# Rows of 768 columns instead of 704 for the intermediate of a quantized feed-forward block

## The chip, the cores and the metric

The kernel runs on one core of a Trainium2 chip. The metric is device time in microseconds (us) of one execution, taken as the median of repeated runs; lower is better. The engines have short names in the profile: PE is TensorE's matmul, PEld its weight load, DVE VectorE, ACT ScalarE, POOL GpSimd and SP the sync engine, which issues the DMAs.

## The reference, cut to what matters

A tensor x of 8 sequences, 1024 rows each, width 256, passes four residual blocks; each adds a function of a layer norm of x:

```python
x = x + linear_attention_layer(layernorm(x))   # block 1, with its own FFN of width 1024 (Gelu)
x = x + relu_ffn(layernorm(x))                 # block 2, width 1024
x = x + softmax_attention(layernorm(x))        # block 3, one head of width 256
x = x + fp4_ffn(layernorm(x))                  # block 4

def fp4_ffn(x):                                # w_gate, w_up: (704, 256), w_down: (256, 704)
    gate = fp4_linear(x, w_gate)
    y = fp4_linear(x, w_up)
    h = silu(gate) * y                         # 704 columns
    return fp4_linear(h, w_down)
```

`fp4_linear` first rounds both operands, in blocks of 16 along the contracted dimension, to a grid of eight magnitudes times the block's scale, and then multiplies. The intermediate `h` has 704 columns, five times 128 and 64. All data are fp32.

## The kernel before

Rows go through in chunks of 128 (64 chunks) and, for blocks 1 and 2, in groups of 4 chunks, the 16 flows. Five generators describe the work: `linear_attention` (block 1's attention, for each flow four `front`s that normalise x, and four `linear_chunk`s), `dense` (the two FFNs of width 1024, with weights streamed from memory in tiles `w_ff`), `softmax_and_fp4` (`soft_chunk`, blocks 3 and 4 of a chunk), and two that prepare weights.

A planner, `Plan`, interleaves them. Each generator yields what its next step needs (an engine, tiles, PSUM banks, a free buffer of a kind); `Plan.run` takes the step that can start first by a table of costs in `Plan.took`, with PE first among equals. `Queue` ties the instructions of each engine to that order, so each engine executes a fixed list and waits in it by semaphores. `TILES` says how many buffers each kind of tile has. Only the order comes from the planner; on the chip every engine runs as soon as its semaphores allow. The planner's price of a matmul follows from the columns of its output alone; it has no term for a change of the array's shape.

Names that occur later:

- `load_x` issues the DMA of a chunk of x into a tile of kind `x`; `front` takes it (statistics `ln_st`, `ln_mv` on DVE, `ln_ve` and `ln_rstd` on POOL, then n on DVE) and gives the buffer back. x has four buffers, one for each chunk of a flow. After its own chunk c, `front` loads chunk c + 4.
- `n0T` is the transposed n of a whole flow, which the projections (`n0T, wqkv`) read once all four fronts are through.
- `soft_chunk` makes, for a chunk, the attention (`n2T`, `qT`, `prob`, `probT`, `vt`), then block 4: gate and up products (`wgT`, `wuT` with `xqT`), the intermediate `hid` of 128x704 in one of three buffers, its rounding by `fp4`, six transposes of `hid` through PSUM into `hqT`, and six matmuls with `wdT` that accumulate the down product, 128x256.
- `hsum`, `qz` and `sc` are operands of block 1's matmuls that use 32 columns or 32 rows of the array at a time.

Around the change, the sixth piece of `hid` has 64 columns. Its transpose therefore gives 64 rows, which are copied out of PSUM by themselves, and the sixth matmul contracts over 64 rows:

```python
INTER_TILES = [(t * P, min(P, INTER - t * P)) for t in range((INTER + P - 1) // P)]
```

Every operation is issued through one helper, so all instructions of the profile stand at line L268 and are told apart by tile names.

Of the kernel before, what the change touches and what calls it, by code (L numbers as in the profile page):

```python
# [9 lines left out]
F32 = mybir.dt.float32  # L10
# [6 lines left out]
P = 128  # L17
D = 256
# [4 lines left out]
INTER = 704  # L23
V_PADS = 5
W_FF = 5
RES = 10
# [3 lines left out]
G = 4  # L30
GT = G * P
LN_EPS = 1e-5
ATT_EPS = 1e-6
BANKS = 8
INTER_TILES = [(t * P, min(P, INTER - t * P)) for t in range((INTER + P - 1) // P)]


# [2 lines left out]


TILES = {
    "x": (4, D, F32),
    "n0": (2, D, F32),
    "lin": (5, D, F32),
    "flow": (9, 512, F32),
# [3 lines left out]
    "soft": (5, D, F32),  # L50
    "prob": (7, 512, F32),
    "rows": (4, D, F32),
    "hid": (3, INTER, F32),
    "q_c": (2, INTER, BF16),
}

# [1 line left out]
class Plan:  # L58
# [27 lines left out]
    def bank(self, tile_):  # L86
        name = tile_.tensor.name
        self.used[name] = 0.0
        if len(self.banks) == BANKS:
            old = min((b for b in self.banks if b not in self.held), key=lambda b: self.used[b])  # L90
# [5 lines left out]
    def banks_free(self, count):  # L96

        if len(self.banks) + count <= BANKS:
            return 0.0
        times = sorted(self.used[b] for b in self.banks if b not in self.held)  # L100
        k = count - (BANKS - len(self.banks)) - 1
        return times[k] if k < len(times) else None
# [9 lines left out]
    def drop(self, *tiles):  # L112

        for tile_ in tiles:
            name = tile_.tensor.name
            kind = self.kind[name]
            self.live[kind].remove(name)
            self.slots[kind].append(self.used[name])

    def slot_free(self, kind):  # L120
        slots, live = self.slots.get(kind, []), self.live.get(kind, ())
        if len(live) + len(slots) < TILES[kind][0]:
            return 0.0
        return min(slots) if slots else None
# [76 lines left out]
    def pe(self, *tiles, **kw):  # L201
        return self.need("tensor", tiles, **kw)

    def dve(self, *tiles, **kw):
        return self.need("vector", tiles, **kw)

    def act(self, *tiles, **kw):
        return self.need("scalar", tiles, **kw)

    def dma(self, *tiles, **kw):  # L210
        return self.need("sync", tiles, **kw)
# [75 lines left out]
def block_stack_kernel(ctx: ExitStack, tc: tile.TileContext, a: dict, out: bass.AP):  # L287
# [20 lines left out]
    plan = Plan(tc, tc.nc)  # L308
    nc, pe, dve, act, dma = plan, plan.pe, plan.dve, plan.act, plan.dma
    x_dram = a["L0_attn_inputs"]  # L310
    B, L, _ = x_dram.shape
    NCH = L // P
    NG = NCH // G

    const = ctx.enter_context(tc.tile_pool(name="const", bufs=1))
# [4 lines left out]
    ps = ctx.enter_context(  # L320
        tc.tile_pool(name="ps", bufs=BANKS, space=bass.MemoryType.PSUM)
    )


    def mm_bank():
        bank = ps.tile([P, 512], F32, tag="bank", name="bank")
        plan.bank(bank)
        return bank

    def tr_bank():  # L330
        return mm_bank().rearrange("p (k t) -> p k t", k=4)
# [6 lines left out]

    def make(kind, name=None):
        bufs, width, dtype = TILES[kind]  # L340
        t = wk.tile([P, width], dtype, tag=kind, name=name or kind, bufs=bufs)
        plan.take(kind, t)
        return t

    def kept(shape, name, bufs):
        t = big.tile(shape, F32, tag=name, name=name, bufs=bufs)
        return t

    def small(shape, name, bufs=4):
        t = sm.tile(shape, F32, tag=name, name=name, bufs=bufs)  # L350
        return t
# [17 lines left out]
    ident = const.tile([P, P], F32, name="ident")  # L369
# [59 lines left out]
    for i in range(V_PADS):  # L429
        v = const.tile([P, H, 32], F32, name=f"v_pad{i}")  # L430
        nc.gpsimd.memset(v, 0.0)
        v_pads.append(v)


    def load_x(c):
        x = make("x")
        s, i = divmod(c, NCH)
        nc.sync.dma_start(out=x, in_=x_dram[s, i * P : (i + 1) * P, :])
        return x

    xs = {c: load_x(c) for c in range(G)}

    wqkv = const.tile([P, 2, 3 * D], F32, name="wqkv")
    bqk1 = const.tile([P, 4], F32, name="bqk1")
# [27 lines left out]
    wgT = const.tile([P, 2, INTER], F32, name="wgT")  # L472
    wuT = const.tile([P, 2, INTER], F32, name="wuT")
    wdT = const.tile([P, len(INTER_TILES), D], F32, name="wdT")


    def ln_stats(src):
# [10 lines left out]
    def layernorm(kind, src):  # L488
        mean, rstd = ln_stats(src)
        dst = yield from fresh(kind, dve(rstd), "n")  # L490
        nc.vector.tensor_scalar(dst, src, mean, rstd, ALU.subtract, ALU.mult)
        return dst
# [11 lines left out]
    def turned(srcs):  # L504

        bank = tr_bank()
        for i, src in enumerate(srcs):
            nc.tensor.transpose(bank[:, i, :], src, ident)
        return bank[:, : len(srcs), :]

    def halves(t):
        return [t[:, 0:P], t[:, P : 2 * P]]
# [51 lines left out]
    def fp4_weights():  # L564
        pieces = []
        for name, dstT in (("L1_ffn_w_gate", wgT), ("L1_ffn_w_up", wuT)):
            for r0, rows in INTER_TILES:
                turns = [(dstT[:, k, r0 : r0 + rows], k * P, P) for k in range(2)]
# [94 lines left out]
    def head_sums(prods):  # L663

        bank = mm_bank()[:, :P]
        for b, prod in enumerate(prods):
            for t in range(G):
                nc.tensor.matmul(
                    bank[32 * t : 32 * t + 32, :],
                    lhsT=hsum[:, b, :],  # L670
                    rhs=prod[:, t * P : (t + 1) * P],
                    start=b == 0,
                    stop=b == 3,
                    skip_group_check=True,
                )
        return bank
# [20 lines left out]
    def running(out, cur, carry, b, first, last):  # L697
# [16 lines left out]
    count = {  # L714
        "halves": 0,
        "dense": 0,
        "acc": 0,
        "res": 0,
        "v": 0,
        "scored": 0,  # L720
        "attended": 0,
        "linear": 0,
# [27 lines left out]
    def linear_group(p):  # L750
# [8 lines left out]

        def front(i):  # L760
            c = p * G + i
            x = xs.pop(c)
            yield dve(x, when=lambda: count["res"] < RES)
            count["res"] += 1
            rc = groups[p]["res"][i] = kept([P, D], "res", RES)
            n0 = yield from layernorm("n0", x)
            plan.drop(x)
            nc.gpsimd.tensor_tensor(rc, n0, bo, ALU.add)
            yield pe(n0, banks=1)
            bank = turned(halves(n0))  # L770
            plan.drop(n0)
            yield act(bank)
            nc.scalar.copy(n0T[:, :, i * P : (i + 1) * P], bank)
            fronts.append(i)
            if c + G < B * NCH:
                need = dma()
                need.fresh = "x"
                yield need
                xs[c + G] = load_x(c + G)

        fronts = []
        yield dve(at=p, when=lambda: count["v"] == p * G)
# [7 lines left out]
        for b in (2, 0, 3, 1):  # L790
            yield pe(n0T, banks=1)
            bank = mm_bank()
            for k in range(2):
                nc.tensor.matmul(
                    bank,
                    lhsT=wqkv[:, k, b * P : (b + 1) * P],
                    rhs=n0T[:, k, :],
# [20 lines left out]
        bank = head_sums(prods)  # L818
# [8 lines left out]
        for n, b in enumerate((2, 0, 3, 1)):  # L827
# [12 lines left out]
        bank = head_sums(prods)  # L840
# [11 lines left out]
        bank = mm_bank()[:, 0:1]  # L852
        nc.tensor.matmul(
            bank, lhsT=front_rows, rhs=total, start=True, stop=first
# [8 lines left out]
        ahead = small([P, 1], "ahead", 2)  # L863
# [24 lines left out]
        bank = tr_bank()  # L888
# [323 lines left out]
    def soft_chunk(cc):  # L1212
        s, c = divmod(cc, NCH)
        g, i = divmod(c, G)
# [4 lines left out]
        bank = mm_bank()  # L1219
        for e in range(2):  # L1220
            for k in range(2):
                nc.tensor.matmul(
                    bank[:, e * P : (e + 1) * P],
                    lhsT=wqk[:, k, e * P : (e + 1) * P],
                    rhs=n2T[g][:, k, i * P : (i + 1) * P],
# [10 lines left out]
        for kb in range(NG):  # L1236
            yield pe(qT, banks=1)
            bank = mm_bank()
            plan.keep(bank)
            for e in range(2):  # L1240
                nc.tensor.matmul(
                    bank, lhsT=qT[:, e, :], rhs=n2T[kb][:, e, :], start=e == 0, stop=e == 1
# [19 lines left out]
        for kb in range(NG):  # L1262
            yield pe(prob[kb], banks=1, at=at + 0.25)
            bank = turned([prob[kb][:, j * P : (j + 1) * P] for j in range(G)])
# [9 lines left out]
        bank = mm_bank()  # L1274
        for j in range(NCH):
            nc.tensor.matmul(
                bank[:, :D],
                lhsT=probT[j // G][:, j % G, :],
                rhs=vt[j // G][:, j % G, :],
# [12 lines left out]
        bank = turned(halves(n))  # L1292
# [3 lines left out]
        hid = None  # L1296
        for j0 in range(0, INTER, INTER // 2):
# [3 lines left out]
            for bank, wT in ((gb, wgT), (ub, wuT)):  # L1301
                for k in range(2):
                    nc.tensor.matmul(
                        bank,
                        lhsT=xqT[:, k, :],
                        rhs=wT[:, k, cols],
# [3 lines left out]
            if hid is None:  # L1310
                hid = yield from fresh("hid", act(gb))
# [8 lines left out]
        hqT = []  # L1320
        for half in range(2):
            yield pe(hid, banks=1, at=at + 0.75)
            tiles = INTER_TILES[4 * half : 4 * half + 4]
            bank = tr_bank()
            for k, (f0, rows_) in enumerate(tiles):
                nc.tensor.transpose(bank[:rows_, k, :], hid[:, f0 : f0 + rows_], ident)
            hqT.append((yield from fresh("prob", act(bank), "hqT")))
            hqT[half] = hqT[half].rearrange("p (k t) -> p k t", k=4)
            if half == 0:
                nc.scalar.copy(hqT[0], bank)  # L1330
            else:
                for k, (f0, rows_) in enumerate(tiles):
                    nc.scalar.copy(hqT[1][:rows_, k, :], bank[:rows_, k, :])
        yield pe(*hqT, banks=1)
        bank = mm_bank()
        for k, (f0, rows_) in enumerate(INTER_TILES):
            nc.tensor.matmul(
                bank[:, :D],
                lhsT=hqT[k // 4][:rows_, k % 4, :],
                rhs=wdT[:rows_, k, :],  # L1340
                start=k == 0,
                stop=k == len(INTER_TILES) - 1,
            )
# [63 lines left out]
```

## Time and profile before

| what | value |
|---|---|
| median of 6 runs | 2788.08 us (2783.82 to 2788.32) |
| the profiled execution | 2788.23 us |
| its span, first to last instruction | 2786.5 us |
| mean granted TensorE clock | 0.982 |
| busy: PE, DVE, ACT, POOL | 95%, 70%, 45%, 20% |
| ACT table loads | 314, 1283 ns each |
| `wdT, hqT` matmul records | 768, of them 128 with 64 rows |
| eviction of `hqT`, first half | 128x512, 585 ns each |
| eviction of `hqT`, second half | 128x128, 266 ns, and 64x128, 263 ns |

A row of groups names engine, operation, the tile written and those read, for PE the rows*columns of the array, the shape and the count; then busy time and mean time of one in ns, then the idle time of the engine just before and what ended it. Matmuls are pipelined and the profile models their ends, so the duration of one record is longer than the distance from its start to the next start. A matmul in fp32 leaves two records, a transpose one.

### The profile page before, as it was taken

What the parts mean: (1) busy time and instruction counts of PE and PEld (TensorE: products, weight loads), DVE (VectorE), ACT (ScalarE), POOL (GpSimd) and SP (SyncE); (2) the same over time, 40 slices, a digit from 0 to 9 for tenths busy, and PEclk for the clock granted to TensorE, in tenths of its full rate; (3) what the DMA queues carried; (4) which work ended last, traced back from release to release, by engine and by line L of the source; (5) the groups of instructions that cost most, each with busy time, mean ns of one, the idle gap of its engine ahead of it and who ended that gap; (6) DMA issues with size and microseconds to landing.
All of it is one profiled execution on the core that took longest, in us unless ns stands there. A gap on an engine that the chain in (4) does not pass through costs nothing.

```text
span 2786.5 us, 42805 instructions
## 1 busy us (share of the span) xinstructions
PE 2647.9 (95%) x15276; PEld 2019.3 (72%) x15276; DVE 1950.9 (70%) x4403; ACT 1255.3 (45%) x2482; POOL 557.9 (20%) x1100
## 2 busy tenths in 40 slices
PE   3978999999999999999999999999999999999997
PEld 1767777777777777777777777777777777777665
DVE  6877676785867768586685867678586766846565
ACT  2424343545444363544545455354544445444342
POOL 1323222121221211122121221212122121111000
PEclk7989999999999999999999999999999999999998
DMA  3234232222323222231222322132232312222000
GB/s 106 79 94 135 76 97 65 89 66 74 97 63 92 70 73 75 77 106 57 84 70 69 98 72 93 52 98 65 71 93 67 97 60 78 71 73 85 21 12 14
DMA packets 283204, 211.43 MB, mean 76 GB/s; under 512 B 23921, under 2 KB 270705, under 8 KB 282993
## 3 DMA queue, kind: packets, MB, share of 16 engines
q1 hardware_dynamic: 282992, 208.71, 25.0%
q8 instruction: 122, 2.00, 0.3%
q14 instruction: 90, 0.73, 0.1%
HBM read 189.74 MB, written 18.87 MB: 75 GB/s over the span
## 4 chain that ended last, share of the span: by engine, by line
PE 76%; DVE 13%; DMA 4%; ACT 4%; issue 2%; POOL 1%; SPq 1%; DVEq 0%; ACTq 0%; POOLq 0%
PE bank L268 76%; DVE prod L268 4%; DMA spread<-packed 2%; ACT L268 2%; DVE n L268 1%; DVE hid L268 1%; DVE spread L268 1%; DMA w_ff<-in_L_ffn_w_dram 1%; DVE ln_st L268 1%; ACT q_c L268 1%; DMA packed<-flow 1%; DVE u L268 1%; DVE x_amax L268 1%; SPq L268 1%; DVE div L268 0%
## 5 line engine op out<-in xcount | busy, mean ns | idle before, releaser
L268 PE MATMUL bank<-half,w_ff 128*128 128x256 f32 x2048 | 535.6, 384 | 16.6 <-DMA w_ff<-in_L_ffn_w_dram 13.4
L268 PE MATMUL bank<-w_ff,hidden 128*128 128x256 f32 x2048 | 527.2, 382 | 0.0
L268 PEld LDWEIGHTS bank<-half,w_ff 128*128 128x128 f32 x2048 | 381.2, 192 | 88.4 <-issue 26.0
L268 ACT ACT_TABLE_LOAD x314 | 402.9, 1283 | 78.2 <-PE bank L268 69.5
L268 PEld LDWEIGHTS bank<-w_ff,hidden 128*128 128x128 f32 x2048 | 368.1, 191 | 67.1 <-issue 24.2
L268 POOL TENSOR_SCALAR ln_ve<-ln_mv 128x1 f32<-128x1 f32 x384 | 89.1, 232 | 1320.6 <-DVE ln_mv L268 1309.7
L268 ACT ACTIVATE hidden<-bank,c_L_ffn_b 128x256 f32<-128x256 f32 x256 | 121.2, 473 | 339.9 <-PE bank L268 339.5
L268 PE MATMUL bank<-n2T,qT 128*128 128x512 f32 x512 | 241.6, 594 | 1.0 <-ACT qT L268 1.0
L268 PE MATMUL bank<-vt,probT 128*128 128x256 f32 x1024 | 234.1, 382 | 2.1 <-DVE probT L268 2.1
L268 DVE TENSOR_TENSOR hid<-hid,bank 128x352 f32<-128x352 f32 x128 | 65.8, 514 | 241.2 <-PE bank L268 160.3
L268 POOL TENSOR_TENSOR ln_rstd<-ln_ve,neghalf 128x1 f32<-128x1 f32 x384 | 225.9, 588 | 32.0
L268 PEld LDWEIGHTS bank<-vt,probT 128*128 128x128 f32 x1024 | 194.7, 192 | 42.6 <-issue 11.7
L268 DVE TENSOR_TENSOR sc<-bank,triu 128x512 f32<-128x512 f32 x256 | 161.9, 681 | 54.8 <-PE bank L268 54.8
L268 PE MATMUL bank<-wdT,hqT 128*128 128x256 f32 (+1 forms) x768 | 193.5, 394 | 0.8 <-ACT hqT L268 0.8
L268 ACT ACTIVATE hidden<-bank,c_L_attn_b 128x256 f32<-128x256 f32 x256 | 121.4, 474 | 146.0 <-PE bank L268 144.5
L268 PE MATMUL bank<-wgT,xqT 128*128 128x352 f32 x512 | 177.5, 469 | 1.6 <-ACT xqT L268 1.5
L268 PE MATMUL bank<-wuT,xqT 128*128 128x352 f32 x512 | 174.5, 464 | 0.0
L268 PEld LDWEIGHTS bank<-wdT,hqT 128*128 128x128 f32 (+1 forms) x768 | 141.5, 193 | 42.2 <-issue 23.7
L268 POOL TENSOR_TENSOR xr<-xr,b_L_attn_ln_b 128x256 f32<-128x256 f32 x64 | 54.3, 869 | 488.6 <-DMA xr<-in_L_attn_inputs_dram 488.6
L268 PEld LDWEIGHTS bank<-n2T,qT 128*128 128x128 f32 x512 | 93.0, 190 | 72.4 <-issue 63.2
L268 PEld LDWEIGHTS bank<-wuT,xqT 128*128 128x128 f32 x512 | 98.5, 192 | 55.2 <-issue 1.7
L268 PEld LDWEIGHTS bank<-wgT,xqT 128*128 128x128 f32 x512 | 92.7, 190 | 47.6 <-issue 12.8
(174 smaller groups left out, 4381.3 us busy)
## 6 DMA issues: line engine op xcount, KB each, us to landing
w_ff<-in_L_attn_W_dram SPq DMA_DIRECT2D x512, 128.0 KB
w_ff<-in_L_ffn_w_dram SPq DMA_DIRECT2D x512, 128.0 KB
spread<-packed SPq DMA_DIRECT2D x96, 256.0 KB
x<-in_L_attn_inputs_dram SPq DMA_DIRECT2D x64, 128.0 KB
xr<-in_L_attn_inputs_dram SPq DMA_DIRECT2D x64, 128.0 KB
rows<-res SPq DMA_DIRECT2D x64, 128.0 KB
rows<-rows SPq DMA_DIRECT2D x64, 128.0 KB
out_dram<-y SPq DMA_DIRECT2D x64, 128.0 KB
```

The lines of the kernel that those rows point to most:

```text
L268: ins = method(*args, **kw)
```

## The change

The tiles of the intermediate get 768 columns, whose last 64 are zeros, and the last 64 rows of the sixth tile of `wdT` are zeros too. Then all six transposes are of 128x128, the second half of `hqT` is evicted by one copy of 128x256 instead of two copies, and all six matmuls contract over 128 rows. Gate, up and the rounding still work on 704 columns.

So that the zeros are written once, the three `hid` tiles become fixed tiles, zeroed in their last columns at the start, and `make` hands out the one that was used longest ago (`Plan.oldest`). The room comes from `x`, which has three buffers instead of four. With three, the first three chunks are loaded at the start, `front` loads chunk c + 3 after its own, and a front waits until its chunk has been loaded.

```diff
@@ -32,6 +32,7 @@
 LN_EPS = 1e-5
 ATT_EPS = 1e-6
 BANKS = 8
+INTER_PAD = -(-INTER // P) * P
 INTER_TILES = [(t * P, min(P, INTER - t * P)) for t in range((INTER + P - 1) // P)]
 
 
@@ -40,7 +41,7 @@
 
 
 TILES = {
-    "x": (4, D, F32),
+    "x": (3, D, F32),
     "n0": (2, D, F32),
     "lin": (5, D, F32),
     "flow": (9, 512, F32),
@@ -50,7 +51,7 @@
     "soft": (5, D, F32),
     "prob": (7, 512, F32),
     "rows": (4, D, F32),
-    "hid": (3, INTER, F32),
+    "hid": (3, INTER_PAD, F32),
     "q_c": (2, INTER, BF16),
 }
 
@@ -116,6 +117,14 @@
             kind = self.kind[name]
             self.live[kind].remove(name)
             self.slots[kind].append(self.used[name])
+
+    def oldest(self, kind, tiles):
+
+        live = self.live.get(kind, ())
+        return min(
+            (t for t in tiles if t.tensor.name not in live),
+            key=lambda t: self.used.get(t.tensor.name, 0.0),
+        )
 
     def slot_free(self, kind):
         slots, live = self.slots.get(kind, []), self.live.get(kind, ())
@@ -338,6 +347,10 @@
 
     def make(kind, name=None):
         bufs, width, dtype = TILES[kind]
+        if kind == "hid":
+            t = plan.oldest(kind, hids)
+            plan.take(kind, t)
+            return t
         t = wk.tile([P, width], dtype, tag=kind, name=name or kind, bufs=bufs)
         plan.take(kind, t)
         return t
@@ -431,6 +444,12 @@
         nc.gpsimd.memset(v, 0.0)
         v_pads.append(v)
 
+    hids = []
+    for i in range(TILES["hid"][0]):
+        h = const.tile([P, INTER_PAD], F32, name=f"hid{i}")
+        nc.gpsimd.memset(h[:, INTER:], 0.0)
+        hids.append(h)
+
 
     def load_x(c):
         x = make("x")
@@ -438,7 +457,7 @@
         nc.sync.dma_start(out=x, in_=x_dram[s, i * P : (i + 1) * P, :])
         return x
 
-    xs = {c: load_x(c) for c in range(G)}
+    xs = {c: load_x(c) for c in range(TILES["x"][0])}
 
     wqkv = const.tile([P, 2, 3 * D], F32, name="wqkv")
     bqk1 = const.tile([P, 4], F32, name="bqk1")
@@ -472,6 +491,7 @@
     wgT = const.tile([P, 2, INTER], F32, name="wgT")
     wuT = const.tile([P, 2, INTER], F32, name="wuT")
     wdT = const.tile([P, len(INTER_TILES), D], F32, name="wdT")
+    nc.gpsimd.memset(wdT[INTER_TILES[-1][1] :, len(INTER_TILES) - 1, :], 0.0)
 
 
     def ln_stats(src):
@@ -759,8 +779,9 @@
 
         def front(i):
             c = p * G + i
+            yield dve(when=lambda: c in xs and count["res"] < RES)
             x = xs.pop(c)
-            yield dve(x, when=lambda: count["res"] < RES)
+            yield dve(x)
             count["res"] += 1
             rc = groups[p]["res"][i] = kept([P, D], "res", RES)
             n0 = yield from layernorm("n0", x)
@@ -772,11 +793,12 @@
             yield act(bank)
             nc.scalar.copy(n0T[:, :, i * P : (i + 1) * P], bank)
             fronts.append(i)
-            if c + G < B * NCH:
+            ahead = c + TILES["x"][0]
+            if ahead < B * NCH:
                 need = dma()
                 need.fresh = "x"
                 yield need
-                xs[c + G] = load_x(c + G)
+                xs[ahead] = load_x(ahead)
 
         fronts = []
         yield dve(at=p, when=lambda: count["v"] == p * G)
@@ -1321,23 +1343,17 @@
         for half in range(2):
             yield pe(hid, banks=1, at=at + 0.75)
             tiles = INTER_TILES[4 * half : 4 * half + 4]
-            bank = tr_bank()
-            for k, (f0, rows_) in enumerate(tiles):
-                nc.tensor.transpose(bank[:rows_, k, :], hid[:, f0 : f0 + rows_], ident)
+            bank = turned([hid[:, f0 : f0 + P] for f0, _ in tiles])
             hqT.append((yield from fresh("prob", act(bank), "hqT")))
             hqT[half] = hqT[half].rearrange("p (k t) -> p k t", k=4)
-            if half == 0:
-                nc.scalar.copy(hqT[0], bank)
-            else:
-                for k, (f0, rows_) in enumerate(tiles):
-                    nc.scalar.copy(hqT[1][:rows_, k, :], bank[:rows_, k, :])
+            nc.scalar.copy(hqT[half][:, : len(tiles), :], bank)
         yield pe(*hqT, banks=1)
         bank = mm_bank()
-        for k, (f0, rows_) in enumerate(INTER_TILES):
+        for k in range(len(INTER_TILES)):
             nc.tensor.matmul(
                 bank[:, :D],
-                lhsT=hqT[k // 4][:rows_, k % 4, :],
-                rhs=wdT[:rows_, k, :],
+                lhsT=hqT[k // 4][:, k % 4, :],
+                rhs=wdT[:, k, :],
                 start=k == 0,
                 stop=k == len(INTER_TILES) - 1,
             )
```

## The prediction

> **What bounds the kernel now.** I read the page first: busy shares, then the chain that ended last. The profiled execution took 2788.23 us with a span of 2786.5 us, so 1.7 us lies around the span; the median of the six runs is 2788.08 us, 0.15 us less.
>
> ```profile
> PE 2647.9 (95%) x15276; PEld 2019.3 (72%) x15276; DVE 1950.9 (70%) x4403; ACT 1255.3 (45%) x2482; POOL 557.9 (20%) x1100
> ...
> PE 76%; DVE 13%; DMA 4%; ACT 4%; issue 2%; POOL 1%; SPq 1%; DVEq 0%; ACTq 0%; POOLq 0%
> ```
>
> TensorE is busy for 95% and carries 76% of the chain. An average hides stages, so next come windows: up to the first down product (432 us), the middle, and the last stretch, where only block 4 is left.
>
> ```profile
> 0.00:432.00 432.00, 347.65 (x2240) 268.20 (x2241) 313.00 (x718) 155.90 (x348) 110.07 (x212) 0.91 0.34 98
> 432.00:2585.00 2153.00, 2121.09 (x12309) 1627.62 (x12308) 1514.42 (x3408) 1028.22 (x1983) 437.95 (x867) 1.00 0.26 77
> 2585.00:2787.00 202.00, 179.21 (x730) 123.49 (x728) 123.45 (x278) 71.22 (x152) 9.93 (x22) 0.95 0.04 14
> ```
>
> The columns are window, length, then busy time and records of PE, PEld, DVE, ACT, POOL. In the middle PE is busy for 2121 of 2153 us (98.5%) at full granted clock: a us of PE time saved there is a us of the span, unless another engine becomes late. In the start (80%) and the end (89%) chains of several engines decide. The same windows restricted to the down product's tile wdT hold 0, 648 and 120 of its 768 matmul records; twelve are one chunk (each fp32 matmul is two records), so 0, 54 and 10 of the 64 chunks.
>
> Then the groups by shape. Array rows*columns stand before the shapes:
>
> ```profile
> L268 PE MATMUL bank<-wdT,hqT 128*128 128x256 f32 x640 | 153.3, 388 | 0.8 <-ACT hqT L268 0.8
> L268 PE MATMUL bank<-ident,hid 128*128 128x128 f32 x320 | 56.0, 276 | 6.1 <-DVE hid L268 6.1
> L268 PE MATMUL bank<-wdT,hqT 64*128 64x256 f32 x128 | 44.7, 429 | 0.0
> L268 PE MATMUL bank<-ident,hid 128*64 128x128 f32 x64 | 17.6, 275 | 0.0
> ```
>
> The 64-row piece is no cheaper than a full one; it is dearer. These means contain the pipeline's latency, so the price is read from starts, in PE's timeline:
>
> ```profile
> 1503.75 1.03 PE L268 MATMUL bank<-half,w_ff 128*128 128x256 f32 x4
> 1504.62 2.95 PE L268 MATMUL bank<-wdT,hqT 128*128 128x256 f32 x12
> 1507.49 1.13 PE L268 MATMUL bank<-w_ff,hidden 128*128 128x256 f32 x4
> 1508.46 1.03 PE L268 MATMUL bank<-half,w_ff 128*128 128x256 f32 x4
> ...
> 1519.02 3.62 PE L268 MATMUL bank<-vt,probT 128*128 128x256 f32 x16
> 1522.48 1.03 PE L268 MATMUL bank<-half,w_ff 128*128 128x256 f32 x4
> ...
> 1534.94 0.38 PE L268 MATMUL bank<-ident,hid 128*128 128x128 f32 x2
> 1535.16 1.03 PE L268 MATMUL bank<-w_ff,hidden 128*128 128x256 f32 x4
> 1536.03 0.38 PE L268 MATMUL bank<-ident,n 128*128 128x128 f32 x2
> 1536.24 1.03 PE L268 MATMUL bank<-half,w_ff 128*128 128x256 f32 x4
> 1537.11 2.95 PE L268 MATMUL bank<-wdT,hqT 128*128 128x256 f32 x12
> 1539.99 0.44 PE L268 MATMUL bank<-ident,n 128*128 128x128 f32 x2
> 1540.26 1.03 PE L268 MATMUL bank<-w_ff,hidden 128*128 128x256 f32 x4
> ```
>
> The reader is to see four things. Sixteen full records (vt, probT) take 1522.48 - 1519.02 = 3.46 us, 0.216 us each. Twelve of a down product, whose last two have 64 rows, take 2.87 and 2.88 us where 12 x 0.216 = 2.59 us would do. The group after it is late too: four records in 0.97 us against 0.87, a transpose pair in 0.27 against 0.21. The second half of hid, whose second transpose has shape 128*64, takes 0.22 us, the same as the full pair of n.
>
> **What the change does, part by part.** *The down product (gain).* Single records in the trace show where the excess lies: the last 128-row record holds PE for 0.309 us until the first 64-row record starts, the two 64-row ones for 0.320 and 0.306, where 0.216 is the pace. Excess 0.093 + 0.104 + 0.090 = 0.287 us a chunk, so 64 x 0.287 = 18.4 us. The first record behind it loses another 0.104 us if it is a product and 0.056 us if a transpose; of the 64 down products 23 are followed by a product, 40 by transposes, one by nothing: 23 x 0.104 + 40 x 0.056 = 4.6 us. Together 23.0 us. With 128 rows everywhere there is no change of shape at this place and I take the excess as gone.
>
> The Trainium skill ("TensorE: Matmul & The Clock Gate", Why this matters for your kernels, the row on small K) says that a matmul with 32 rows takes as long as one with 128, and its section on LDWEIGHTS that rows do not matter to the load. By that rule alone nothing would be gained on PE and the sum would stay at 2788 us. "TensorEngine Tiling (Array Packing)", Key Properties, says that changing the tiling mode drains the TensorE; that agrees with 0.309 against 0.216 us here, but it would charge the 128*64 transposes as well, and the trace shows 0.22 us for such a pair, no charge. The measurement decides in both cases.
>
> *The transposes of hid.* 128*64 becomes 128*128 at the same pace (0.22 us a pair): nothing. Bounds: 64 x 0.056 us = 3.6 us either way, by the loss of a transpose after a change of shape.
>
> *The order.* The planner replans everything, since TILES changed. I counted changes of array shape in PE's order of both programs: 429 before, 308 after. That is 121 fewer, not the 128 of the 64 chunks, so seven more arise elsewhere (hsum, qz, sc groups that no longer touch). Seven at 0.093 + 0.104 = 0.197 us give 1.4 us back: 23.0 - 1.4 = 21.6 us. PE's instruction count is the same.
>
> *ACT.* Two evictions of hqT (266 and 263 ns) become one of 128x256, which in this trace takes 368 ns (xqT): 64 x 0.16 = 10 us less. The order also has 284 table loads instead of 314: 30 x 1.283 = 38.5 us less. ACT is busy 45%, so this is off the path, except where PE waits for it: in the middle window PE waits 14.2 us for ACT's prob. Bounds for the rearranged waits: all of it gone (-14), or as much again (+14). I take 0, since the same tasks still alternate in nearly the same order.
>
> *x in three buffers instead of four.* This is what pays for the 64 more columns. The fourth x of each flow (512 rows) now loads only after the first front's normalisation has freed a buffer. In DVE's order that chunk's statistics stand 11 to 25 instructions behind the freeing one (once 66) in the 16 flows, where before it was over 100. At DVE's mean of 1950.9/4403 = 0.44 us that is 5 to 11 us, against an xr load of 2.3 us from issue to landing plus 0.4 us of issue. It is covered unless SP holds the load behind a w_ff load that waits for PE. Queued behind a late one are DVE's next instructions, and PE behind those. Bounds: 0, and 16 x 2.4 = 38 us if each flow's wait were as long as DVE's mean wait for spread (38.5 us in 16 waits) and PE stood still for it. Those 38.5 us exist already, and all of PE's waits for DVE in the middle window are 17 us, so most of such a wait is covered: I take +1 us. At the start the fourth x is issued behind six w_ff DMAs, some 17 us later than before; but SP is done issuing its first loads at 25.5 us in any case, and DVE's first scan at 32.8 us waits for ACT, so I take 0 there, with -1 to +3.
>
> *Memsets.* Four on POOL before the first statistics, at most 0.53 us each (the v_pad row, a larger tile). POOL idles 4.8 us there: nothing. Without that cover at most 2 us.
>
> *Where PE time doesn't bind.* 10/64 of 21.6 us = 3.4 us are saved in the end stretch. PE carries about 76% of the chain there, so 0.8 us of it is lost again.
>
> Sum: 2788.1 - 21.6 + 1 + 0.8 = 2768.3; I say 2768.
>
> **Rivals.** *(a) Half of it comes back.* PE runs 1% faster against unchanged DVE and ACT, the plan doesn't know of it, and its waits grow by half of the gain: 2768 + 11 = 2779. For: DVE is busy 70% and runs in order. Against: in the middle, PE waits only 31 us in all now. *(b) Rows don't matter.* The excess belongs to the tail of an accumulation group, not to its shape, and stays: then the order alone acts, 2787 to 2790. Against: vt, probT ends its accumulation with no excess. *(c) Slower: the x ring.* Each flow waits 2.4 us for its fourth x and PE stands for it: 16 x 2.4 - 21 = +17, 2805 us. It turns the sign from 1.3 us a flow. For: the load is the one transfer that loses its lead. Against: the 5 to 11 us above. *(d) More than the sum.* Half of PE's waits for prob go with the table loads: 2761.
>
> **How the numbers follow.** Forecast case 0.68, (d) 0.08, (a) 0.12, (b) 0.05, (c) 0.07. A measurement of this kernel tells about 0.2% (5.6 us) from no change, so faster means below 2782.5. The forecast, (d) and nearly all of (a) lie there: 0.87. (b) is no change: 0.05; the rest of (a) joins it, 0.06 in all. (c) gives 0.07. The range: below, (d) with some us more, 2757; above, (a) with the start's +3, 2782. It leaves out (b) and (c) and little else.
>
> **What would show it.** In the profile after: wdT, hqT is one group of 768 records with 128*128; twelve start-to-start take 2.60 us and the group behind keeps 0.87; in the middle PE stays at 98% busy; PE's busy time falls by about 20 us; ACT has 284 table loads. If (c) is right, DVE's waits name DMA x, with 16 of them over 1 us; if (a), PE's waits for DVE and ACT in the middle rise from 31 us towards 40. I am wrong if twelve full records still take 2.87 us, or if a wait for x stands in the chain.

## The result, and the profile after

The changed kernel takes 2791.29 us (median; before, run on the same chips, 2783.69). The ratio is 1.0023, 95% interval 1.0017 to 1.0029: slower by 0.23%, 6.4 us by the ratio and 7.6 by the medians, where 2768 us had been forecast. (The forecast's sum starts from 2788.1, the median of six runs; over 75 runs the kernel before is at 2783.7.) The profiled execution, 2784.39 us, is one of the shortest; a second profile of the same kernel, taken with the experiments, has a span of 2797.7 us.

From the page of the changed kernel: span, busy times, shares of the chain, and two groups.

```profile
span 2782.7 us, 42675 instructions
...
PE 2627.9 (94%) x15276; PEld 2026.3 (73%) x15276; DVE 1953.0 (70%) x4403; ACT 1210.4 (43%) x2388; POOL 570.1 (20%) x1104
...
PE 82%; DVE 9%; DMA 3%; ACT 3%; issue 1%; POOL 1%; SPq 1%; POOLq 0%; DVEq 0%; ACTq 0%
...
L277 ACT ACT_TABLE_LOAD x284 | 364.4, 1283 | 70.5 <-PE bank L277 66.5
...
L277 PE MATMUL bank<-wdT,hqT 128*128 128x256 f32 x768 | 177.8, 381 | 1.0 <-ACT hqT L277 1.0
```

The down product is one group of 768 full records, and PE's busy time fell by 20.0 us (2647.9 to 2627.9). The span fell by only 3.8 us, and the median rose. PE therefore stands idle longer. The windows (columns as before) say where:

```profile
0.00:432.00 432.00, 346.39 (x2250) 267.62 (x2251) 312.37 (x723) 156.32 (x348) 112.24 (x218) 0.92 0.33 97
432.00:2585.00 2153.00, 2113.18 (x12318) 1639.58 (x12317) 1518.05 (x3404) 985.40 (x1902) 447.98 (x865) 1.00 0.26 77
2585.00:2783.00 198.00, 168.36 (x711) 119.11 (x709) 122.55 (x277) 68.71 (x138) 9.93 (x22) 0.96 0.04 14
```

In the middle PE was busy 2121.1 of 2153 us before and is busy 2113.2 now. A PE that loses 18 us less there (54/64 of 21.6) and waits no more would have put some 0.8% more records through; it put through as many (12309 before, 12318 now). That PE is still busy for 98% of the middle, as the prediction asked for, thus says little. PE's timeline in that window shows both halves of the story:

```profile
2028.09 2.75 PE L277 MATMUL bank<-wdT,hqT 128*128 128x256 f32 x12
2030.68 0.38 PE L277 MATMUL bank<-ident,n 128*128 128x128 f32 x2
2030.90 1.89 PE L277 MATMUL bank<-w_ff,hidden 128*128 128x256 f32 x8
2034.82 0.41 PE L277 MATMUL bank<-ident,n 128*128 128x128 f32 x2 [2.02 <-DVE n L277]
```

Twelve records of the down product now take 2030.68 - 2028.09 = 2.59 us instead of 2.87, and the transposes behind them 0.22 us. Then PE waits 2.02 us for n. DVE's timeline of the same stretch says why n is late:

```profile
2030.01 0.18 DVE L277 BATCH_NORM_AGGREGATE ln_mv<-ln_st 128x2 f32<-128x6 f32 x1
2032.35 0.69 DVE L277 TENSOR_TENSOR spread<-k,spread 128x512 f32<-128x512 f32 x1 [2.16 <-DMA spread<-packed]
2033.08 1.28 DVE L277 TENSOR_TENSOR_SCAN prod<-one,carry_w,spread 128x512 f32<-128x512 f32 x1
2034.28 0.39 DVE L277 TENSOR_SCALAR n<-res,ln_mv,ln_rstd 128x256 f32<-128x256 f32 x1
```

n stands behind the product with spread and its scan, and that product waits 2.16 us for a transfer. In DVE's whole order n<-res stands right behind such a scan four times; in the kernel before, once.

To see the whole, I priced each run of equal PE records at its pace (0.216 us for a record of 256 columns, and so on), added 0.093 us for each change of array shape and 0.104 (product) or 0.056 us (transpose) for the first record of 64 or 128 rows behind one, and called what is left between starts a stall. In us:

| profiled run | changes of shape | stalls to 432 us | 432 to 2585 | behind 2585 | span |
|---|---|---|---|---|---|
| before | 65.2 | 102.1 | 46.2 | 33.4 | 2786.5 |
| changed kernel | 43.3 | 102.9 | 61.3 | 37.2 | 2782.7 |
| changed kernel, again | 43.3 | 110.2 | 67.8 | 37.3 | 2797.7 |

(The priced work itself is 2522.3 us before and 2520.2 in the first profile of the changed kernel; some 17 us of the span lie outside PE's records.) Changes of shape cost 21.9 us less, and stalls grew by 20 and by 34 us.

### The profile page after: what moved, and what is told of

The parts are those of the page before. It is cut to its first block, busy times and chain, and to the rows that moved or that the text cites. A ratio compares the mean times of both kernels' runs of the same rounds, so it can differ in the third digit from the quotient of the medians.

```text
span 2782.7 us, 42675 instructions
## 1 busy us (share of the span) xinstructions
PE 2627.9 (94%) x15276; PEld 2026.3 (73%) x15276; DVE 1953.0 (70%) x4403; ACT 1210.4 (43%) x2388; POOL 570.1 (20%) x1104
## 4 chain that ended last, share of the span: by engine, by line
PE 82%; DVE 9%; DMA 3%; ACT 3%; issue 1%; POOL 1%; SPq 1%; POOLq 0%; DVEq 0%; ACTq 0%
PE bank L277 82%; DVE prod L277 2%; DMA spread<-packed 1%; DVE hid L277 1%; DVE n L277 1%; ACT L277 1%; DVE ln_st L277 1%; SPq L277 1%; DMA w_ff<-in_L_ffn_w_dram 1%; DVE u L277 0%; DVE spread L277 0%; ACT qz L277 0%; DVE x_amax L277 0%; DVE mx L277 0%; POOL ln_rstd L277 0%
## 5 line engine op out<-in xcount | busy, mean ns | idle before, releaser
L277 DVE TENSOR_TENSOR sc<-bank,triu 128x512 f32<-128x512 f32 x256 | 160.8, 682 | 48.9 <-PE bank L277 47.9
L277 PE MATMUL bank<-wdT,hqT 128*128 128x256 f32 x768 | 177.8, 381 | 1.0 <-ACT hqT L277 1.0
L277 PEld LDWEIGHTS bank<-wdT,hqT 128*128 128x128 f32 x768 | 145.5, 191 | 23.1 <-ACT hqT L277 1.9
L277 ACT ACTIVATE hid<-bank 128x352 f32<-128x352 f32 x128 | 59.3, 463 | 178.5 <-PE bank L277 176.8
```

Of the source, the lines that this page charges most:

```text
L277: ins = method(*args, **kw)
```

## The experiments

All ratios are to the kernel before, with 95% intervals. "Full rows" in a kernel with `hid` of 704 columns means that the sixth piece is taken from columns 576 to 704 and meets 64 rows of zeros in `wdT`, so nothing of the result changes.

**Rows and order apart.** Three theories: O, the new order costs what full rows bring; W, PE's freed time turns into waits in any order; X, the late fourth x costs. The first kernel has before's order, instruction for instruction, with full rows (its main lines; the weights of the sixth piece and the second copy of `hqT` are moved to match):

```diff
+    tc.nc.gpsimd.memset(wdT[: P - INTER_TILES[-1][1], len(INTER_TILES) - 1, :], 0.0)
...
-                nc.tensor.transpose(bank[:rows_, k, :], hid[:, f0 : f0 + rows_], ident)
+                nc.tensor.transpose(bank[:, k, :], hid[:, f0 + rows_ - P : f0 + rows_], ident)
...
-                lhsT=hqT[k // 4][:rows_, k % 4, :],
-                rhs=wdT[:rows_, k, :],
+                lhsT=hqT[k // 4][:, k % 4, :],
+                rhs=wdT[:, k, :],
```

> The old order of every engine is kept, x keeps four buffers, hid stays at 704 columns and both copies of hqT stay; only the sixth piece becomes full: it is transposed from columns 576 to 703, and its tile of wdT has zeros in the first 64 rows. Theory O (the new order costs what the full rows bring): the full rows alone bring what the prediction summed for the 64 chunks, 23 us less a little at the end, so 2783.7 - 22 = 2762 us (2758 to 2767), ratio 0.992. Theory W (freed PE time turns into waits for DVE and ACT in any order): ratio 0.998 to 1.002, 2778 to 2789 us, with PE's waits in the middle up by 15 us or more.

Measured: 2767.48 us, ratio 0.9935 (0.9918 to 0.9952), 0.5 us above O's range and far below W's. Full rows bring 17.7 us, W falls. The reverse, the changed kernel's order with the sixth matmul on 64 rows again:

```diff
-                lhsT=hqT[k // 4][:, k % 4, :],
-                rhs=wdT[:, k, :],
+                lhsT=hqT[k // 4][:rows_, k % 4, :],
+                rhs=wdT[:rows_, k, :],
```

> The changed kernel with its order of every engine, padded tiles and all; only the sixth matmul contracts over 64 rows again. Theory O: the new order costs about 7.6 + 22 = 29 us against the kernel before, so 2813 us (2807 to 2818), ratio 1.010. Theory W: PE time is not what decides, so this takes as long as the changed kernel, 2791 us (2786 to 2795), ratio 1.001 to 1.004.

Measured: 2810.32 us, 1.0086 (1.0069 to 1.0103). The new order, with the three x, the single copy and the fixed tiles that come with it, costs 0.9%, about 25 us, and full rows bring 18 us in it as well. Then before with only x changed to three buffers, with the new `front`:

```diff
-    "x": (4, D, F32),
+    "x": (3, D, F32),
...
-    xs = {c: load_x(c) for c in range(G)}
+    xs = {c: load_x(c) for c in range(TILES["x"][0])}
```

> The kernel before with three buffers of x in place of four and the new front, 64 rows and hid of 704 columns kept; the planner makes a third order of its own. Theory X (the late fourth x is the loss, whatever the order): 2784 + 20 to 29 us, so 2804 to 2813, ratio 1.007 to 1.010, with DVE waiting for the DMA of x in most of the 16 flows. Theory O with the loss in the order that the cheaper copy of hqT brought: 2779 to 2792 us, ratio 0.998 to 1.003.

Measured: 2778.03 us, 0.9978 (0.9967 to 0.999). Three x by themselves cost nothing; X falls as put. The changed kernel beside them:

> The changed kernel once more, unchanged, for a second profile beside the others on this chip: 2791 us by its median so far (2785 to 2797), ratio 1.002; its first profile was of a short execution (2784.4 us). All theories expect the same; the second profile is to show which waits differ between a short and a long execution.

Measured: 2791.6 us, 1.0025 (1.0012 to 1.0037).

**Which edit makes the costly order.** The planner sees three inputs change: x has three buffers, one copy of `hqT` is cheaper than two, and it charges GpSimd with four memsets. Each was tried, always with full rows. Three x, two copies:

> The order of the run with three x (2778), instruction for instruction, with six full rows in the down product (the sixth piece taken from columns 576 to 704, so that its first 64 rows meet zeros). If the full rows are worth the same in any order (theory O: 18 us), 2760 (2754 to 2766), the fastest so far. If what full rows bring is lost wherever the cores wait more (theory W), 2770 to 2778.

Measured: 2766.51 us, 0.9931 (0.9918 to 0.9944): in this order full rows bring some 13 us (6 to 20 by the two intervals). Four x, one copy, as an edit to the first kernel:

```diff
-            if half == 0:
-                nc.scalar.copy(hqT[0], bank)
-            else:
-                for k, (f0, rows_) in enumerate(tiles):
-                    nc.scalar.copy(hqT[1][:, k, :], bank[:, k, :])
+            nc.scalar.copy(hqT[half][:, : len(tiles), :], bank[:, : len(tiles), :])
```

> The planner has before's four x; only the one copy of hqT (0.2 us of planned ScalarE time less, 64 times) makes it plan anew. Theory C (the single copy makes the costly order): 2785 to 2795. Theory M (no single edit is to blame: each new plan falls where it falls, and this change's was a bad one): anywhere from 2755 to 2790, and below 2772 speaks for M against C.

Measured: 2770.59 us, 0.9951 (0.9939 to 0.9963). The single copy by itself is not to blame either. One copy in before's order, held by charging the planner for two:

> Before's order held, full rows, four x, and hqT's second half taken in one copy instead of two, while the planner is charged for two. If the one copy is harmless in itself (theories C and M): 2765 to 2768, no more than 2 us below the 2767.5 with two copies. If the copy itself costs (a later release of its bank or of hqT): 2775 or more.

Measured: 2772.53 us, 0.9956 (0.9944 to 0.9968), between what was expected of a harmless copy and of a costly one. Its interval just meets that of two copies (0.9918 to 0.9952), so a cost of the copy itself of some 5 us stays open. The changed kernel's order, with a fourth buffer behind x on the chip, whose room comes from `hid` (704 columns again, full rows):

```diff
-    "hid": (3, INTER_PAD, F32),
+    "hid": (3, INTER, F32),
...
-        t = wk.tile([P, width], dtype, tag=kind, name=name or kind, bufs=bufs)
+        t = wk.tile([P, width], dtype, tag=kind, name=name or kind, bufs=bufs + (kind == "x"))
```

> The changed kernel's order, instruction for instruction on all engines, but with a fourth buffer behind x, so that the order is planned with three and the load needs to wait for one less. Theory X (in that order the late x is what costs): the 18 us of VectorE's waits for x go, 2772 to 2780. Theory O (the order's own arrangement costs, x is hidden): 2788 to 2793, the waits for x gone or changed into others.

Measured: 2797.88 us, 1.0041 (1.0029 to 1.0053). DVE's waits of this kernel in the middle still name x:

```profile
DVE ln_st L277 <- DMA x<-in_L_attn_inputs_dram: 20.2, 9, 3.8
```

(waiting engine and tile, releaser, us in total, times, longest). With a buffer to spare the wait is as long as in the changed kernel (18.1 us): the load's place in SP's order makes it, not the buffer.

Next the planned memsets. In the changed kernel they are issued past the planner:

```diff
-        nc.gpsimd.memset(h[:, INTER:], 0.0)
+        tc.nc.gpsimd.memset(h[:, INTER:], 0.0)
...
-    nc.gpsimd.memset(wdT[INTER_TILES[-1][1] :, len(INTER_TILES) - 1, :], 0.0)
+    tc.nc.gpsimd.memset(wdT[INTER_TILES[-1][1] :, len(INTER_TILES) - 1, :], 0.0)
```

> The changed kernel with its four memsets of zeros issued past the planner, so that the planner no longer charges GpSimd with them (three times 0.48 and once 0.73 us of planned time at the start). Same tiles, same three x, same single copy, same zeros; only the order differs, from PE's third place on. Theory G (this charge is what makes the costly order): 2765 to 2772. Theory M (each of the three planner inputs shifts the order by some us, no one of them is the cause): anywhere from 2765 to 2792. If the three x and the one copy together make the costly order: 2788 to 2795.

Measured: 2791.16 us, 1.0024 (1.0013 to 1.0035): another order, the same time. In the other three the planner is charged, and nothing is issued for it:

```diff
+    for _ in range(3):
+        plan.free["gpsimd"] = plan.free.get("gpsimd", 0.0) + 0.4 + 1.3e-3 * 64
...
+    plan.free["gpsimd"] = plan.free.get("gpsimd", 0.0) + 0.4 + 1.3e-3 * D
```

> Before's four x and two copies, full rows, and the planner charged with the changed kernel's four memsets (nothing else is issued for it): a new order by the charge alone. Theory G: 2785 to 2795. Theory M: anywhere from 2760 to 2790; under 2775 speaks against G as a cause by itself.

> Four x, one copy, full rows, the charge: the changed kernel's planner inputs except for the x. Without the charge this was 2770.6. Theory G: 2785 to 2795. Theory M: anywhere from 2760 to 2790.

> Three x, two copies, full rows, the charge: the changed kernel's planner inputs except for the copy. Without the charge this was 2766.5. Theory G: 2785 to 2795. Theory M: anywhere from 2760 to 2790.

Measured: 2769.32 us, 0.9947 (0.9931 to 0.9963); 2770.4 us, 0.9945 (0.9927 to 0.9962); 2761.6 us, 0.9921 (0.9905 to 0.9937). The charge reorders PE from its third place on and costs nothing, G falls. What is left is three x and one copy together (theory I), or the fixed tiles of 768 columns (F), which all costly runs shared. The changed kernel with the two copies put back, in the order of the 2761.6 us run:

> The changed kernel with one thing undone: hqT's second half is copied in two pieces again, all else kept (three x, three fixed tiles of 768 columns with zeros, the planned memsets). Its order is, instruction for instruction on every engine that matters, that of the charged run with three x and two copies (2761.6). Theory I (three x and one copy together make the costly order): 2758 to 2767. Theory F (the fixed tiles of 768 columns cost, by the buffer that is taken or by their zeros): 2785 to 2795.

Measured: 2766.34 us, 0.993 (0.9919 to 0.9942). The costly orders with `hid` from a rotating pool:

> The changed kernel's order, instruction for instruction, but hid comes from a rotating pool of 704 columns as before, the sixth piece is taken from columns 576 to 704, and no memset of hid is issued (the planner is charged for them). Theory I: 2788 to 2795, as the changed kernel. Theory F: 2762 to 2770.

> As the run before, without the charge: the order of the changed kernel with unplanned memsets (2791.2), hid from the pool. Theory I: 2786 to 2794. Theory F: 2762 to 2770.

Measured: 2796.24 us, 1.0035 (1.0023 to 1.0047), and 2794.35 us, 1.003 (1.0019 to 1.0041). I holds and F falls:

| full rows, ratio to before | two copies | one copy |
|---|---|---|
| four x | 0.9935; charged 0.9947 | 0.9951; charged 0.9945; in before's order 0.9956 |
| three x | 0.9931; charged 0.9921; fixed tiles 0.9930 | 1.003; charged 1.0035; fixed tiles 1.0023 to 1.0025, with a fourth x behind 1.0041 |

Nothing here is additive: neither edit costs more than some 0.2% alone, together they cost 1%. One combination was not run, the costly order with two copies on the chip; against the copy itself as the cause speak the run with one copy in before's order and the last run below, which has one copy too.

**What the costly order costs by.** The largest of PE's waits in the middle, first of the changed kernel, then with two copies:

```profile
PE bank L277 <- DVE n L277: 8.7, 8, 2.3
PE bank L277 <- ACT prob L277: 8.4, 10, 1.0
PE bank L277 <- DVE kv L277: 6.4, 6, 1.7
PE bank L277 <- DVE v L277: 5.3, 12, 0.6
```

```profile
PE bank L277 <- DVE prod L277: 9.8, 6, 2.5
PE bank L277 <- DVE n L277: 7.1, 20, 0.7
PE bank L277 <- DVE sc L277: 6.6, 13, 0.9
PE bank L277 <- DVE kv L277: 1.9, 6, 0.3
```

The longest wait for n is 0.7 us with two copies and 2.3 us with one; for kv 0.3 and 1.7. The stalls by stage, as above:

| profiled run | changes of shape | to 432 us | 432 to 2585 | behind 2585 | span |
|---|---|---|---|---|---|
| before's order, full rows | 42.2 | 96.2 | 50.6 | 29.8 | 2758.2 |
| changed kernel, two copies | 42.4 | 107.2 | 47.9 | 29.4 | 2765.6 |
| four x, one copy | 43.2 | 104.3 | 46.5 | 35.8 | 2768.4 |
| changed kernel's order, pooled hid | 43.3 | 102.9 | 65.9 | 38.8 | 2791.5 |

Against two copies, the changed kernel's 61.3, 67.8 and 65.9 us (three profiles of its order) are 13 to 20 us more in the middle, and 37.2 to 38.8 us some 8 to 9 us more at the end. One copy alone has 6 of those at the end, and none in the middle. At the end PE waits 10.9 us for DVE's hid and 8.3 us for n in the changed kernel, 5.4 and 3.5 us with two copies.

DVE's waits for transfers in the middle go along with this: spread and x together 65 to 70 us in the orders with three x and one copy, 26 to 47 us in the other orders with full rows so far. In the changed kernel, then with four x and one copy:

```profile
DVE spread L277 <- DMA spread<-packed: 47.1, 12, 5.6
DVE ln_st L277 <- DMA x<-in_L_attn_inputs_dram: 18.1, 9, 3.3
```

```profile
DVE spread L268 <- DMA spread<-packed: 47.2, 12, 5.8
```

Theory D took these waits for the cause. The second kernel, at 0.9951, already speaks against their amount: it waits as long for spread. PE's timeline says more. Of the 21 waits in the changed kernel, three stop PE at once: those of 2.21, 2.41 and 2.16 us (DVE goes on at 712.0, 1373.2 and 2032.4 us) with n right behind the scan, for which PE waits 2.07, 2.27 and 2.02 us. The six of 5.0 to 5.6 us for spread and all nine for x are followed by no PE wait of over 0.3 us in the next 25 us, and neither are the six of over 5 us with four x and one copy. So it is n's place that costs: it stands behind such a scan four times in every run with three x and one copy except the last one below, once in every other. The three waits of 1.7 us for kv have no transfer ahead of them. For the one at 1613.56 us, DVE has no pause of over 0.1 us from 1601.32 us until kv is made, behind the rounding of another chunk's n:

```profile
1611.25 1.37 DVE L277 TENSOR_TENSOR n<-n,q_c 128x256 f32<-128x256 f32 x2
1612.65 0.43 DVE L277 TENSOR_TENSOR n<-n,x_s 128x256 f32<-128x256 f32 x1
1613.00 0.42 DVE L277 TENSOR_TENSOR kv<-bank,bdiag 128x256 f32<-128x256 f32 x1
```

These six waits for n and kv make 11.6 us of PE's time, and the clock that is lost behind such waits (see the last section) 2 to 5 us more than with two copies; the other waits differ both ways. To test D, the load of spread was cut loose from the store before it, in the costly order and, as a control, in the order with two copies:

```diff
-                    tensor=flat.tensor,
-                    offset=flat.offset + 8 * b * GT,
+                    tensor=x_dram.tensor,
+                    offset=x_dram.offset + 8 * b * GT,
```

> The changed kernel and its order, instruction for instruction; only the loads of spread read x's rows in DRAM in place of what the transfer before them has just stored (the linear attention is thereby computed from other numbers), so they need not wait for that store. Theory D (VectorE's 47 us of waits for spread, with n and kv queued behind them, are what costs in this order): 2770 to 2780, the waits for spread under 15 us and PE's for n and kv mostly gone. Theory A (the arrangement costs in other places too, in the end above all): 2784 to 2791.

> The same with two copies (2766.3 with the true loads, VectorE's waits for spread 30 us): the control. Theory D: little to gain here, 2760 to 2766. Theory A: as much gained here as in the run before.

Measured: 2779.8 us, 0.9993 (0.9981 to 1.0004), and 2752.95 us, 0.9892 (0.9874 to 0.9909): 8 and 11 us below the same kernels with true loads (by the ratios 1.0023 and 0.993). DVE's waits in the middle of the first:

```profile
DVE spread L277 <- DMA spread<-in_L_attn_inputs_dram: 47.7, 12, 6.0
...
DVE ln_st L277 <- DMA x<-in_L_attn_inputs_dram: 19.6, 9, 3.4
```

The wait that was to go is still there (47.1 us in the changed kernel). SP's queue explains it; its timeline in the changed kernel, ahead of the 2.16 us wait shown above:

```profile
2026.11 0.56 SPq L277 DMA_DIRECT2D packed<-flow  x1
2027.42 0.89 SPq L277 DMA_DIRECT2D w_ff<-in_L_ffn_w_dram  x2
2028.68 2.46 SPq L277 DMA_DIRECT2D spread<-packed  x4
```

The load follows its store by 2.57 us, behind two loads of w_ff, and DVE goes on at 2032.35, 3.67 us after the first issue. With the link cut it follows by 2.30 us (2019.12 to 2021.42): only 0.27 us was the store's, and the rest is issue and transfer. So the edit left the wait in place, and these two runs do not decide on D, though the first lies in its range. Both gain about as much, as A said, and the gain shows ahead of 432 us (stalls there 102.9 to 90.8, and 107.2 to 98.0 us).

The last run changes what the planner believes of a transfer, in the changed kernel as it is:

```diff
-            cost, after = 0.4, 2.2
+            cost, after = 0.4, 3.6
```

> The changed kernel with one planner constant changed: a transfer is expected 3.6 us after its issue in place of 2.2, so that VectorE's tasks that need one are put later. Own order, three x, one copy. Theory D: 2765 to 2780, since n no longer stands behind a spread that is still under way. Theory A or M: anywhere from 2765 to 2800.

Measured: 2753.34 us, 0.989 (0.9875 to 0.9905), below all that was expected, the fastest of the kernels that keep the whole computation, 1.1% below before. Its waits in the middle, DVE's for transfers and PE's longest:

```profile
DVE spread L277 <- DMA spread<-packed: 8.2, 13, 1.0
```

```profile
PE bank L277 <- DVE kv L277: 7.8, 7, 1.1
PE bank L277 <- DVE u L277: 6.9, 6, 1.2
PE bank L277 <- ACT prob L277: 5.9, 8, 1.0
```

DVE waits 8.2 us for transfers instead of 65, none of it for x, and PE's stalls in the middle are 35.3 us instead of 61 to 68; at the end they are 39.0 us. With three x and one copy the costly order is thus not forced. In it n stands behind a scan once, and n is not among the waits of PE in the middle, while kv is still waited for, 1.1 us at the longest. That it gains by n's place fits; but this order differs from the others everywhere, so it is argued, not shown. The end, as costly as in the other kernels with one copy, is untouched by it.

## Why the prediction was wrong

- *The down product.* Right. Predicted: 23.0 us, 21.6 with the seven new changes of shape. Traces: changes of shape 65.2 to 43.3 us, 21.9 less; twelve records in 2.59 us. On the clock, full rows bring 17.7 us in the old order (13 to 23 by its interval), 18 us in the new one and some 13 in the order with three x and two copies. Rival (b) is refuted, and so is the sum of 2788 us that followed from equal times of 64 and 128 rows.
- *The order: the step that failed.* "I take 0, since the same tasks still alternate in nearly the same order", with bounds of 14 us either way. Measured with 64 rows: +25 us; with full rows, against the order with two copies, 13 to 20 us of stalls in the middle and 8 to 9 at the end. The count of changes of shape compared the two orders by one property, and the bound was made from a single wait of before (prob); the waits that came were for n, kv and v. Prob's even fell, 14.2 to 8.4 us, as (d) hoped.
- *x in three buffers.* Predicted +1 us; the edit alone gave -6 us, its own new order included. Rival (c) had the right sign by the wrong means: DVE waits for x ten times, 19.2 us in all, not in each of 16 flows, none of the nine in the middle is followed by a stop of PE, and a fourth buffer brings nothing back.
- *One copy.* It was booked as 10 us less of ACT, off the path. As an input to the planner it decides the sign, together with three x.
- *Memsets and the transposes of hid.* Nothing, as said; the charge for the memsets alone reorders everything and costs nothing.
- *Rival (a).* Its sign was there, PE's listed waits in the middle rose from 31.3 to 38.8 us. Its cause was not: in before's order they rise only to 34.4 us with the same faster PE.
- *The end.* Predicted +0.8 us; the stalls there grew by 3.8 us, and shrank by 3.6 in before's order.

Open stays why the planner, given three x and one copy, falls into this order. Its long waits end at 714.5, 1375.7 and 2034.8 us for n and at 952.5, 1613.6 and 2272.9 us for kv, some 660 us apart, while with two copies small waits for kv (0.3 us) return every 327 us.

## What to carry to other kernels

Where an order is planned from costs, an edit has two prices: its instructions, and the new order, which here was worth from -12 to +30 us at the same work and could not be read from the old trace. Hold the old order, and each edit's own price can be measured by itself; then try the edits singly and in pairs, since two harmless ones can meet badly. And where an engine that works through a fixed list waits for a transfer, look at what stands right behind: of 21 such waits here the fifteen that include the longest were followed by no stop of PE, and three shorter ones cost it 2 us each. One other value of one planner constant was worth more than the change (2753 us); since it was one try among orders that lie over 40 us apart, luck may have a part in it.

## What the runs showed of the hardware

A wait of 1.6 to 3.1 us on PE can cost more than itself. In the changed kernel PE waits 1.73 us for kv:

```profile
1611.39 0.44 PE L277 MATMUL bank<-ident,n 128*128 128x128 f32 x2
1613.56 1.89 PE L277 MATMUL bank<-wv,n2T 128*128 128x256 f32 x4 [1.73 <-DVE kv L277]
```

and the windows behind it show the granted clock (third column from the right) at half:

```profile
1612.00:1614.00 2.00, 0.44 (x2) 0.39 (x3) 1.34 (x4) 0.24 (x1) 0.51 (x1) 0.93 0.22 72
1614.00:1616.00 2.00, 1.91 (x7) 1.13 (x5) 0.51 (x2) 0.09 (x1) 0.22 (x1) 0.50 0.00 0
1616.00:1618.00 2.00, 2.00 (x7) 1.72 (x8) 2.00 (x4) 0.28 (x1) 0.00 (x0) 0.71 0.00 0
```

Clock missing in these windows, 0.07 x 2 + 0.50 x 2 + 0.29 x 2 = 1.7 us, is lost again: the four records at 1613.56 take 1.68 us to the next start, where 4 x 0.216 = 0.86 would do. The middle has two such stretches in the changed kernel, four when it was run again, three with pooled hid, one to four in all profiles of the costly orders, and none to two in before and the other orders that keep the whole computation. In the middle of every profile, each began within 2.1 us of the end of a PE wait of 1.6 us or more; many such waits were followed by none. The wait of 2.02 us at 2034 was followed by none, one of 2.31 us at the same place in the other run was. The Trainium skill ("TensorE: Matmul & The Clock Gate", HAM oscillation — how this bites in real kernels) warns of idle gaps over about 3.4 us; here about half of that was enough at times.
